# Self-attention on one core: the softmax denominators of a unit move from the front of the next unit's first run of 32-column products to the back of its second run

## The chip, the cores and the metric

The kernel runs on one core of a Trainium2 chip. The core has a matrix engine (TensorE, PE in the profile, with its weight loads shown apart as PEld), a vector engine (DVE), an activation engine (ACT), a general engine (GpSimd, POOL), and DMA queues, most of them issued by SyncE (SPq) and some by ACT (ACTq). The engines run side by side, each takes its own instructions in order, and they wait for one another through semaphores. The metric is the time on the device in microseconds (us), the median of several executions; lower is better. Before the change it is 2229.88 us, the median of three runs (2228.8 to 2230.53).

## The reference, cut to what matters

Four sequences of 1024 tokens and 512 channels go through a decoder layer (causal self-attention, cross-attention over 64 context tokens, a feed-forward part) and then through a gated fusion. The change touches only the causal self-attention, which has 16 heads of 32 channels:

```python
xn1 = _ln(x, g1, be1)
q, k, v = ...                                  # 16 heads of 32 channels
scores = jnp.einsum('bhtd,bhsd->bhts', q, k) / scale       # scale = 32 ** -0.5
scores = jnp.where(mask, scores, -jnp.inf)                 # causal
attn = jax.nn.softmax(scores, axis=-1)
out  = jnp.einsum('bhts,bhsd->bhtd', attn, v)
```

A softmax row is exp(score - row maximum), divided by its sum. The kernel applies that division late: it first multiplies the exponentials with v, and separately adds the exponentials over all keys; that sum is the denominator.

## The kernel before, in words

**Units.** Self-attention is cut into 32 units: 4 sequences, times 4 groups of 4 heads, times 2 sets of 4 query tiles (a tile is 128 queries, so a unit has 512 query columns). In sequence 0, group 0, the two sets are tiles 0 to 3 and 4 to 7; everywhere else they are (0, 1, 6, 7) and then (2, 3, 4, 5), so two kinds of units take turns. In this text the first is the *wide* kind (it looks at 8 key blocks of 128 keys) and the second the *middle* kind (6 key blocks).

**What a unit does.** `maxima` (products `s`, L673) finds row maxima ahead of time. `attend` then handles the key blocks `kb` in a hand-written order (`o7` = 0, 7, 2, 1, 3, 6, 4, 5 for the wide kind, `o5` = 0, 5, 1, 4, 2, 3 for the middle kind). For each block `exps` makes the scores again, transposed (TensorE, tile `st`, L729, in a PSUM pool of three banks), takes exponentials on ACT into SBUF tiles `pT` (L734; the first block's go to two of the four `total` buffers, the others to a ring of seven), and, for a block on the diagonal, zeroes the masked half on POOL with affine_select (L742). A block `kb` covers only the query columns that may see it, from `first_col[kb]` to 512: in the wide kind 512 columns for block 0 and 128 for block 7; in the middle kind 512 for block 0 and 128 for block 5.

**The runs of 32-column products.** Every two blocks, `weigh_all` (L747) multiplies the exponentials with v: four products per block, one per head, each with a stationary operand of 32 columns and up to 512 moving columns (`av`, L759). A product appears as two matmul records in the trace, because the operands are float32. These products are kept together: the first is the *lead*, and the others are tied to come behind it on TensorE and get a high priority (`issue_after`, `high_priority`), so that they normally form one run. After each run POOL adds the blocks' exponentials into the first block's tiles (`weigh`, L783): `held[0]` is both the operand of the first block's products and the accumulator, so the first add of a unit has to wait until those products have read it. When the last block has been added, `held[0]` holds the sums over keys.

**The denominators.** `sums` (L791) makes, for unit u, four more 32-column products with a stationary matrix of ones (`den`, L796), which add `held[0]` over the 128 partitions, into a bank of the `st` pool; then `end` copies the bank to SBUF on ACT (`dens`, L801) and sends it to DRAM by SyncE's queue (`dend`, L804). `attend` returns `sums` as the next unit's `tail`. In the kernel before, unit u+1's first run calls it: the denominators of unit u lead, and the run's own products come behind them. The last unit's denominators are made alone at the end of the phase.

**What sets the order.** `run` (L114) merges three streams of steps (a unit's own steps, the maxima of the units ahead, and the projections of later sequences as filling) by the share that is left of each, and gives each stream a priority. When the program is built, a planner turns this list into one fixed order per engine with its own estimates of when things are ready: on each engine it takes the ready instruction of the highest priority. The chip then runs each engine's order as it is and waits where an operand is late. So a change of one run's lead may change where many other instructions stand.

Of the kernel before, what the change touches and what calls it, by code (L numbers as in the profile page):

```python
# [28 lines left out]
HG = P // DH  # L29
# [22 lines left out]
def decoder_then_fusion(ctx: ExitStack, tc: tile.TileContext, x, ctxT, cols, rows,  # L52
# [385 lines left out]
    def self_attention(ph):  # L438
# [99 lines left out]
        def columns(tiles, n):  # L538

            at = [j for j, tile in enumerate(tiles) if tile // NJ == n]  # L540
            if not at:
                return None
            first = tiles[at[0]] % NJ
            return slice(at[0] * P, (at[-1] + 1) * P), slice(first * P, (first + len(at)) * P)
# [74 lines left out]
        order = list(range(KST))  # L619
# [89 lines left out]
        def attend(u, tail):  # L709


            b, g, h, tiles = units[u]

            order = Z["o%d" % tiles[-1]] if tiles[0] != 4 else Z["o9"]
            first_col = [P * sum(tile < kb for tile in tiles) for kb in range(tiles[-1] + 1)]
            last = order[-1]
            held = {}

            def exps(kb, r, m):

                c0 = first_col[kb]
                w = TG - c0
                if r == 0:
                    tag, bufs = ("total", 4) if kb == order[0] else ("pT", None)
                    held[kb] = [ptp.tile([P, 2, TG], F32, tag=tag, name=f"pT_{u}_{kb}_{i}", bufs=bufs)
                                for i in range(2)]
                st = ps_of["st"][0].tile([P, m, w], F32, tag=ps_of["st"][1], name=f"st_{u}_{kb}_{r}")
                for i in range(m):
                    nc.tensor.matmul(st[:, i], k_at[u, kb // NJ][:KM, r + i, (kb % NJ) * P : (kb % NJ + 1) * P],  # L729
                                     q_at[u][:KM, r + i, c0:], start=True, stop=True)  # L730
                for i in range(0, m, 2):
                    k = min(m, 2)
                    at = (r + i) % 2
                    nc.scalar.activation(held[kb][(r + i) // 2][:, at : at + k, c0:], st[:, i : i + k], AF.Exp,  # L734
                                         scale=-QSCALE)

                done = r + m
                for i in range(HG // 2):
                    if kb in tiles and r < 2 * i + 2 <= done:
                        t = held[kb][i][:, :, c0 : c0 + P]  # L740
                        if i < Z["mp"]:
                            nc.gpsimd.affine_select(out=t, in_=t, compare_op=ALU.is_ge, fill=0.0, base=0,  # L742
                                                    pattern=[[0, 2], [1, P]], channel_multiplier=-1)
                        else:
                            nc.vector.tensor_tensor(t, t, reach.unsqueeze(1).to_broadcast([P, 2, P]), ALU.min)

            def weigh_all(kbs):  # L747

                if kbs[0] == order[0]:
                    held["av"] = ps_av.tile([P, TG], F32, tag="av", name=f"av_{u}")  # L750
                    todo = [(kb, r) for kb in kbs for r in range(HG)[::-1]]
                else:
                    todo = [(kb, r) for kb in kbs[::-1] for r in range(HG)[::-1]]
                if kbs[-1] == last:
                    todo = [(kb, r) for kb in sorted(kbs, key=lambda k: k == last) for r in range(HG)[::-1]]

                def one(kb, r):
                    c0 = first_col[kb]
                    return nc.tensor.matmul(held["av"][r * DH : (r + 1) * DH, c0:],  # L759
                                            v_at[b, g][:, kb, r * DH : (r + 1) * DH],  # L760
                                            held[kb][r // 2][:, r % 2, c0:], start=kb == order[0], stop=kb == last)
                if kbs[0] == order[0] and tail:
                    lead, others, end = tail()
                    others += [lambda at=at: one(*at) for at in todo]
                else:
                    lead, *others = [lambda at=at: one(*at) for at in todo]
                    end = lambda: None
                first = lead().ins
                with tc.issue_after(first), tc.high_priority(offset=Z["hp"]):
                    for product in others:  # L770
                        product()
                end()
                for kb in kbs:
                    weigh(kb)

            def weigh(kb):
                c0 = first_col[kb]
                if kb != order[0]:

                    spare = u + Z["spf"] - len(units)  # L780
                    for i, (t, p) in enumerate(zip(held[0], held[kb])):
                        eng = nc.vector if i and (u == 1 and kb in Z["dv1"] or spare >= 0 and (kb % 2 or spare > 1) or spare < 0 and kb in Z["dv"]) else nc.gpsimd
                        eng.tensor_tensor(t[:, :, c0:], t[:, :, c0:], p[:, :, c0:], ALU.add)  # L783
                if kb == last:
                    avs = outp.tile([P, TG], F32, tag="avs", name=f"avs_{u}", bufs=1)
                    nc.scalar.copy(avs, held["av"])
                    for n in range(NG):
                        if shared := columns(tiles, n):
                            nc.sync.dma_start(av_dram[b, n, g][:, shared[1]], avs[:, shared[0]])

            def sums():  # L791

                den = ps_of[Z["den"]][0].tile([P, TG], F32, tag=ps_of[Z["den"]][1], name=f"den_{u}")

                def product(r):
                    return nc.tensor.matmul(den[r * DH : (r + 1) * DH, :], ones, held[0][r // 2][:, r % 2, :],  # L796
                                            start=True, stop=True)

                def end():
                    dens = outp.tile([P, TG], F32, tag="dens", name=f"dens_{u}", bufs=1)  # L800
                    nc.scalar.copy(dens, den)  # L801
                    for n in range(NG):
                        if shared := columns(tiles, n):
                            nc.sync.dma_start(den_dram[b, n][g * HG : (g + 1) * HG, shared[1]],  # L804
                                              dens[::DH, shared[0]])

                first, *others = [lambda r=r: product(r) for r in range(HG)[::-1]]
                return first, others, end

            groups_of = [order[i : i + Z["grp"]] for i in range(Z["grp0"], len(order), Z["grp"])]  # L810
            if Z["grp0"]:
                groups_of.insert(0, order[: Z["grp0"]])
            due = {sum(len(a) for a in groups_of[: i + 1]) - 1 + Z["lag"]: a for i, a in enumerate(groups_of)}

            steps = []
            for i in range(len(order) + Z["lag"]):
                if i < len(order):
                    kb = order[i]
                    w = TG - first_col[kb]
                    m = TG // w if w <= TG // 2 else 1  # L820
                    steps += [(m * w, lambda kb=kb, r=r, m=m: exps(kb, r, m)) for r in range(0, HG, m)]
                if i in due:
                    kbs = due[i]
                    steps.append((4 * sum(TG - first_col[kb] for kb in kbs), lambda kbs=kbs: weigh_all(kbs)))
            return steps, sums
# [77 lines left out]
        tail, first_late = None, len(units) - AHEAD  # L903
        for u in range(len(units)):
            if u and u + 2 < len(units):
                load_stacks(u + 2, u)
            main, tail = attend(u, tail)
# [4 lines left out]
            if u and u + 2 < len(units) and Z["phi%d" % n]:  # L912
                begun = maxima(u + 2)
                k = Z["phi%d" % n]
                first = begun[: k]
# [11 lines left out]
            else:  # L927
                fill = pieces[u + AHEAD]
            run(main, ahead, fill, speed=(Z["main"], (Z["ahead%d" % n] if u < Z["alf"] else Z["ahead_l"]) if u else Z["a0"], Z["fill"]), sooner=(Z["so0"], Z["so1"], Z["so2"]))
        first, others, end = tail()  # L930
        first()
        for product in others:
            product()
        end()
        switch(None)()
# [613 lines left out]
    for phase in (self_attention, cross_attention, feed_forward):  # L1549
        with ExitStack() as ph:  # L1550
            phase(ph)
# [41 lines left out]
```

## Time and profile before

| what | value |
|---|---|
| median of the runs | 2229.88 us |
| the profiled execution's own time | 2229.15 us |
| its span, first to last instruction | 2227.4 us |
| mean granted TensorE clock | 0.981 |
| PE busy over the span | 2121.6 us (95%) |
| POOL busy over the span | 1070.6 us (48%) |
| the stretch in which unit denominators are made (115 to 970 us) | 855.0 us |
| PE / DVE / ACT / POOL busy in it | 811.4 / 560.6 / 442.4 / 666.0 us |
| denominator products | 256 records, 114.2 to 969.0 us |
| copies of the denominators on ACT | 32, 586 ns each (median) |
| their DMAs in that stretch | 58 of 4 KB and 2 of 8 KB |

The busy time of an engine is the time its instructions took; the rest is idle. The idle time before a group of instructions is put down to whatever ended it (the releaser). TensorE's matmuls overlap, and their ends are modelled, so the distance between the starts of two matmuls tells their price better than their durations do. A waits view lists, for an engine and a line, whom it waited for: total us, how many times, the longest. In a timeline, `x8` means that eight records in a row were merged into one line, and the second column is the time from the first start to the last end.

### The profile page before, as it was taken

How to read it: one execution, taken by the hardware profiler on the slowest of the kernel's cores; microseconds unless marked ns; L12 is line 12 of the kernel's file. 1: busy time of each engine (PE TensorE's matmuls, PEld its weight loads, DVE VectorE, ACT ScalarE, POOL GpSimd, SP SyncE). 2: the span in 40 equal slices, each digit the busy share in tenths (PEclk: the TensorE clock that was granted, in tenths of full speed). 3: DMA queues.
4: the chain of work that ended last, by engine and by line, in shares of the span. 5: the costliest groups of instructions: out<-in, count | busy, mean ns of one | idle time of the engine just before them, and what ended most of it. 6: DMA issues, size and time to landing. Idle time of an engine off the chain costs nothing.

```text
span 2227.4 us, 34074 instructions
## 1 busy us (share of the span) xinstructions
PE 2121.6 (95%) x11736; PEld 1606.5 (72%) x11736; DVE 1255.2 (56%) x2800; ACT 983.7 (44%) x2175; POOL 1070.6 (48%) x1139
## 2 busy tenths in 40 slices
PE   6899999999999999989999998999999999999997
PEld 5667665666666755558888886888887887888785
DVE  6566756765665578666677756341337225431727
ACT  3355545554655455435555565432233324232432
POOL 3178777787878778765555523010115103410414
PEclk9999999999999999999999999999999999999998
DMA  8856766676656467662323214644345525442631
GB/s 251 241 157 172 238 194 206 192 221 191 192 151 189 136 168 221 201 205 67 101 80 104 80 50 154 197 166 141 124 139 207 170 98 202 145 175 85 207 134 48
DMA packets 219427, 356.24 MB, mean 160 GB/s; under 512 B 33516, under 2 KB 101852, under 8 KB 217206
## 3 DMA queue, kind: packets, MB, share of 16 engines
q1 hardware_dynamic: 201548, 333.83, 48.0%
q10 hardware_dynamic: 17706, 20.24, 2.9%
q8 instruction: 93, 1.52, 0.3%
q14 instruction: 80, 0.66, 0.1%
HBM read 242.27 MB, written 111.18 MB: 159 GB/s over the span
## 4 chain that ended last, share of the span: by engine, by line
PE 67%; DMA 10%; DVE 10%; issue 6%; POOL 4%; ACT 3%; SPq 1%; DVEq 0%; ACTq 0%; POOLq 0%
PE ph_f L101 13%; PE acc_f L1331 13%; PE s L673 4%; PE st L729 4%; PE av L759 4%; PE po_c L101 3%; PE pq_x L101 3%; PE pk L101 3%; PE pg_o L101 3%; PE pq L101 3%; PE po_x L101 3%; POOL pT L783 3%; PE pv L101 2%; PE sc_c L86 2%; PE den L796 1%
## 5 line engine op out<-in xcount | busy, mean ns | idle before, releaser
L783 POOL TENSOR_TENSOR pT<-pT,pT 128x256 f32<-128x256 f32 (+3 forms) x369 | 547.4, 1504 | 98.4 <-PE av L759 85.0
L1331 PE MATMUL acc_f<-wf,hs_f 128*128 128x512 f32 x1536 | 384.9, 394 | 7.6 <-DVE hs_f L74 5.9
L734 ACT ACTIVATE pT<-st 128x512 f32<-128x512 f32 (+2 forms) x640 | 317.2, 561 | 158.0 <-PE st L729 101.3
L101 PE MATMUL ph_f<-xn_f,wf 128*128 128x512 f32 x1536 | 381.7, 393 | 3.3 <-DVE xn_f L74 2.6
L1331 PEld LDWEIGHTS acc_f<-wf,hs_f 128*128 128x128 f32 x1536 | 285.0, 188 | 71.0 <-DVE hs_f L74 8.1
L101 PEld LDWEIGHTS ph_f<-xn_f,wf 128*128 128x128 f32 x1536 | 287.8, 189 | 65.0 <-DVE xn_f L74 3.0
L678 DVE CUSTOM_DVE_ANT_0 s<-s,mask 128x512 f32<-128x512 f32 (+3 forms) x512 | 245.8, 502 | 118.8 <-PE s L673 118.0
L673 PE MATMUL s<-ks,qs 96*128 96x512 f32 (+3 forms) x768 | 250.8, 375 | 28.4 <-DVE top L681 8.3
L1310 ACT ACTIVATE ph_f<-ph_f,colv 128x512 f32<-128x512 f32 x128 | 84.4, 659 | 391.3 <-PE ph_f L101 387.2
L74 DVE TENSOR_TENSOR hs_f<-ph_f,hs_f 128x512 fp32r<-128x512 f32 x128 | 87.9, 686 | 285.6 <-ACT hs_f L73 285.6
L729 PE MATMUL st<-qs,ks 98*128 98x256 f32 (+2 forms) x888 | 231.1, 342 | 12.2 <-DMA qs<-mT 6.6
L681 DVE TENSOR_REDUCE top<-s 128x1 f32<-128x512 f32 x256 | 175.6, 686 | 108.5 <-PE s L673 108.1
L673 PEld LDWEIGHTS s<-ks,qs 96*128 96x128 f32 x768 | 140.5, 194 | 107.3 <-DVE top L681 23.1
L729 PEld LDWEIGHTS st<-qs,ks 98*128 98x128 f32 x888 | 150.0, 193 | 65.3 <-ACT pT L734 24.7
L1306 POOL TENSOR_TENSOR y_f<-y_f,row_bf 128x512 f32<-128x512 f32 x32 | 42.0, 1317 | 313.8 <-DMA y_f<-x 253.9
L742 POOL TENSOR_SCALAR_AFFINE_SELECT pT<-pT 128x256 f32<-128x256 f32 x256 | 106.0, 431 | 126.1 <-ACT pT L734 92.6
L759 PE MATMUL av<-pT,v 128*32 128x512 f32 (+3 forms) x1776 | 157.2, 455 | 5.1 <-POOL pT L742 4.6
L1446 POOL TENSOR_TENSOR g_o<-g_o,z_o 128x512 f32<-128x512 f32 x28 | 41.8, 1506 | 175.7 <-DVE g_o L1445 172.9
L101 PE MATMUL pv<-wv,xn_s 128*128 128x256 f32 x768 | 107.5, 290 | 6.7 <-ACT vout L578 5.4
L101 PEld LDWEIGHTS pv<-wv,xn_s 128*128 128x128 f32 x768 | 100.4, 194 | 18.3 <-ACT vout L578 6.0
L1082 POOL TENSOR_TENSOR p_c<-p_c,inv_c 128x512 f32<-128x512 f32 x64 | 68.8, 1076 | 87.1 <-DVE inv_c L1081 65.2
L101 PE MATMUL pk<-xn_s,wk 128*128 128x512 f32 x384 | 104.0, 412 | 1.6 <-ACT xn_s L73 0.8
(220 smaller groups left out, 3397.0 us busy)
## 6 DMA issues: line engine op xcount, KB each, us to landing
wf<-wf2d SPq DMA_DIRECT2D x84, 512.0 KB
ks<-kd SPq DMA_DIRECT2D x96, 256.0 KB
qs<-qd SPq DMA_DIRECT2D x96, 256.0 KB
kd<-k SPq DMA_DIRECT2D x64, 256.0 KB
qd<-q SPq DMA_DIRECT2D x120, 128.0 KB
wf<-wf1d SPq DMA_DIRECT2D x28, 512.0 KB
x<-in_x SPq DMA_DIRECT2D x32, 256.0 KB
wk<-wk SPq DMA_DIRECT2D x16, 512.0 KB
```

Of the source, the lines that this page charges most:

```text
L74: (lo_eng or nc.vector).tensor_tensor(lo, src, hi, ALU.subtract)
L101: nc.tensor.matmul(held["ps"], a_at(a()[i], c), b_at(b()[j], c), start=not bias and c == 0 and k == 0, stop=c == NC - 1 and k == 2)
L673: nc.tensor.matmul(sc[:, :w], q_at[u][:KS, r, j * P : (j + 1) * P], k_at[u, m][:KS, r, :w], start=True, stop=True)
L678: nc.vector.tensor_tensor_reduce(sc[:, :w], sc[:, :w], mask[:, TG - w :], 1.0, TOP, ALU.add, ALU.min, dst)
L681: nc.vector.tensor_reduce(dst, sc, AX.X, ALU.min)
L729: nc.tensor.matmul(st[:, i], k_at[u, kb // NJ][:KM, r + i, (kb % NJ) * P : (kb % NJ + 1) * P], q_at[u][:KM, r + i, c0:], start=True, stop= ...
L734: nc.scalar.activation(held[kb][(r + i) // 2][:, at : at + k, c0:], st[:, i : i + k], AF.Exp, scale=-QSCALE)
L742: nc.gpsimd.affine_select(out=t, in_=t, compare_op=ALU.is_ge, fill=0.0, base=0, pattern=[[0, 2], [1, P]], channel_multiplier=-1)
L759: return nc.tensor.matmul(held["av"][r * DH : (r + 1) * DH, c0:], v_at[b, g][:, kb, r * DH : (r + 1) * DH], held[kb][r // 2][:, r % 2, c0: ...
L783: eng.tensor_tensor(t[:, :, c0:], t[:, :, c0:], p[:, :, c0:], ALU.add)
L1310: nc.scalar.activation(ps, ps, AF.Relu, bias=col("bf1", f))
L1331: mm = nc.tensor.matmul(acc[j], held[f][i0][:, j * P : (j + 1) * P], w[2, f][:, i1], start=f == 0 and m == 0, stop=last and m == 2)
```

## The change

Unit u's denominators are no longer made with unit u+1's first run. `weigh_all` now calls `tail` when it reaches the run that begins with `order[Z["grp"]]`, the third block in the order, which is the second run; the four denominator products are appended to that run's products, so the run's own first product leads and the denominators come last. The copy and the DMAs of the denominators (`end`) move with them. The first run is now led by its own first product: block 0, head 3. `sums` returns one list of products instead of a first one and the others; the four products at the end of the phase stay what they are.

```diff
@@ in weigh_all @@
-                if kbs[0] == order[0] and tail:
-                    lead, others, end = tail()
-                    others += [lambda at=at: one(*at) for at in todo]
-                else:
-                    lead, *others = [lambda at=at: one(*at) for at in todo]
-                    end = lambda: None
+                sums, end = tail() if kbs[0] == order[Z["grp"]] and tail else ([], lambda: None)
+                lead, *others = [lambda at=at: one(*at) for at in todo] + sums
                 first = lead().ins
                 with tc.issue_after(first), tc.high_priority(offset=Z["hp"]):
                     for product in others:
@@ in sums @@
-                first, *others = [lambda r=r: product(r) for r in range(HG)[::-1]]
-                return first, others, end
+                return [lambda r=r: product(r) for r in range(HG)[::-1]], end
@@ at the end of the phase @@
-        first, others, end = tail()
-        first()
-        for product in others:
+        sums, end = tail()
+        for product in sums:
             product()
         end()
```

## The prediction

> **What bounds the kernel now.** I read the busy table by stretches first, then the waits between 115 and 970 us (where the denominators are made), then TensorE's and POOL's timelines around a few first runs, and last the clock at one stall. The busy table for that stretch, and for its best and worst 100 us (columns: stretch, length, busy us and count for PE, PEld, DVE, ACT, POOL, then clock, DMA share, GB/s):
>
> ```profile
> 115.00:970.00 855.00, 811.39 (x5181) 543.08 (x5174) 560.64 (x1521) 442.38 (x881) 665.97 (x670) 0.98 0.65 189
> ```
> ```profile
> 700.00:800.00 100.00, 99.56 (x670) 68.80 (x669) 60.79 (x186) 51.48 (x104) 80.50 (x81) 1.00 0.55 153
> 800.00:900.00 100.00, 90.33 (x521) 58.44 (x519) 80.39 (x186) 54.00 (x108) 80.97 (x72) 0.91 0.72 207
> ```
>
> TensorE is the bound: 811.4 of 855.0 us, so 43.6 us idle in all; POOL is at 78%. The waits of the same stretch:
>
> ```profile
> POOL pT L783 <- PE av L759: 81.9, 27, 7.6
> POOL pT L742 <- ACT pT L734: 75.4, 29, 6.3
> ...
> PEld st L729 <- ACT pT L734: 23.4, 47, 2.7
> ...
> PEld av L759 <- POOL pT L742: 14.0, 31, 0.8
> ...
> PE st L729 <- ACT pT L734: 5.0, 3, 2.4
> PE av L759 <- POOL pT L742: 4.6, 12, 0.6
> ```
>
> and, from the waits of TensorE alone:
>
> ```profile
> PE den L796 <- POOL pT L783: 2.1, 1, 2.1
> ```
>
> The reader sees that the large waits stand on POOL, which has slack: its first add of a unit waits for the unit's first `av` run, 81.9 us in 27 units, 3.0 us each. TensorE's own waits on exponentials and masks are small: 5.0 + 4.6 us, and 2.1 for a denominator. How one wait of the first kind looks, on POOL and then on TensorE, in a middle unit:
>
> ```profile
> 502.19 0.77 POOL L742 TENSOR_SCALAR_AFFINE_SELECT pT<-pT 128x256 f32<-128x256 f32 x2 [0.25 <-ACT pT L734]
> 508.06 3.90 POOL L783 TENSOR_TENSOR pT<-pT,pT 128x256 f32<-128x256 f32 x3 [5.10 <-PE av L759]
> ```
> ```profile
> 502.84 2.92 PE L101 MATMUL pq<-xn_s,wq 128*128 128x512 f32 x12
> ...
> 505.99 1.07 PE L796 MATMUL den<-pT,ones 128*32 128x512 f32 x8
> 506.87 1.26 PE L759 MATMUL av<-pT,v 128*32 128x512 f32 x16
> 508.06 0.61 PE L673 MATMUL s<-ks,qs 96*128 96x256 f32 x2
> ```
>
> The masks were done at 502.96, the last add of the unit before at 501.94; TensorE did 2.9 us of projection and then denominators plus `av`. It was never idle: POOL's 5.10 us were free of charge.
>
> **The price of a run.** Starts on TensorE's timeline, at full clock, to the start of the next other matmul:
>
> ```profile
> 583.12 1.05 PE L796 MATMUL den<-pT,ones 128*32 128x512 f32 x4
> 584.10 0.50 PE L673 MATMUL s<-ks,qs 96*128 96x512 f32 x1
> ...
> 586.36 1.06 PE L759 MATMUL av<-pT,v 128*32 128x512 f32 x8
> 587.35 0.45 PE L729 MATMUL st<-qs,ks 98*128 98x384 f32 x1
> ...
> 588.08 0.43 PE L759 MATMUL av<-pT,v 128*32 128x128 f32 x8
> 588.43 0.33 PE L673 MATMUL s<-ks,qs 96*128 96x128 f32 x1
> ```
>
> Four products of 512 columns take 0.99 us alone, of 128 columns 0.35. So 384 columns are worth 0.64 us, 512 are worth 0.85, and 0.99 - 0.85 = 0.14 us is a fixed price per run. The 505.99 run tests it: 512 + 512 + 128 columns give 0.14 + 1.92 = 2.06; its starts are 2.07 apart. The denominators thus cost 0.85 us in any run, and moving them costs nothing in itself; what counts is how many runs there are.
>
> **The change part by part.** Sum against the profiled execution's own 2229.15 us (span 2227.4 and 1.75 around it), which is 0.73 under the median of 2229.88.
>
> 1. *Four denominator products, 31 times, from the first run to the second.* 31 x 0.85 us leave one place and appear in the other: 0. Where the `st` bank they need is not free when the second run is issued, they become a run of their own: 0.14 each. Before, 4 of the 31 already stand apart from the `av` products, which are then a run. Bounds 0 - 4 x 0.14 = -0.6 and 27 x 0.14 = +3.8; I take half, +1.6.
>
> 2. *The first run has a new lead.* Before, the denominators' lead needed a free `st` bank and the previous unit's finished sums; by then both blocks of the first run were usually ready in the 16 middle units (one run), while in the wide units block 7 stood apart by itself (0.35 us). Now the lead is block 0's own product, which can be placed as soon as block 0 is ready, so that block 5 of the middle units falls behind: 16 x 0.14 = +2.2 at worst; joined in the 15 wide units instead, -2.1. In a middle unit block 0 needs no mask and block 5 does, which favours the split: +1.1.
>
> 3. *The first run loses a cover.* The 0.85 us of denominators let POOL's masks of the new unit finish while TensorE was busy. Those masks often end right at that time (for the denominators at 480.80 the last one of the batch ends at 480.95). The other 126 or so runs have no such cover, and TensorE's wait for a mask is 4.6 us in 12 cases, 0.4 each. By their rate the 31 first runs pay 31 x 12/126 x 0.4 = 1.2; if every one lost the whole cover, 31 x 0.85 = 26. Below nothing is excluded, since the old wait for POOL's sums is counted in 4. The nearest row is the 0.4 us of one wait; I take it in 10 of the 31 units, +4.0, because the masks of the wide units are the last things to come. What is queued behind such a wait is all of TensorE's order, `st` and `s` first.
>
> 4. *POOL starts a unit's adds sooner.* Up to 81.9 us of POOL's waiting can go. POOL was off the path, so what TensorE gets is only its own waits on this chain: 5.0 + 4.6 + 2.1 = 11.7 us at most, and nothing at least, because the `st` waits I looked at come with ACT held up by a DMA (ACT's 0.5 to 4.3 us waits of `vout` for `vd`). I take -1.5.
>
> 5. *What moves with the denominators.* One ACT copy of 0.59 us per unit, later by the distance of the two runs (5 to 10 us), and two DMAs of 4 KB on SyncE's queue, past the loads and stores issued in that time. SyncE already waits 28.8 us for these copies with its later transfers queued behind. Nobody needs the values within 10 us: the inverse is read two units after a sequence's last unit. The `held[0]` buffers are four, two units' worth, so they too have 10 us to spare. 0; without that cover, a late stack load stalls TensorE by what its longest such wait shows, 3.5 us (`s` for `qd`, in the waits of the whole span).
>
> 6. *The fixed order is planned anew.* Every lead that moves shifts the work around it. TensorE's idle time per 100 us varies from 0.4 to 9.7 us in the present order with the same kinds of work. I take +2 for the following: a stall also costs clock. Bounds -8 and +12, an estimate from that spread, as no row prices a new order.
>
> The clock, shown by the stall at 531 us (columns as in the first table):
>
> ```profile
> 528.60:531.60 3.00, 0.78 (x5) 0.47 (x4) 1.27 (x4) 1.73 (x4) 0.00 (x0) 1.00 0.25 96
> 531.60:535.60 4.00, 3.88 (x18) 1.03 (x18) 1.77 (x6) 2.08 (x5) 1.13 (x3) 0.60 0.84 306
> ```
>
> A 2.24 us wait is followed by a granted clock of 0.60, and denominators plus 512 columns took 3.43 us instead of 1.85: 1.6 us on top of the stall. So two new stalls of this size would cost 7.7 us by the row. The Trainium skill, "TensorE: Matmul & The Clock Gate", section "Why this matters for your kernels", asks only that gaps stay under about 3 us. By that rule two 2.24 us stalls would cost 4.5 us and no clock; this trace disagrees with it, and the trace decides.
>
> Sum: 1.6 + 1.1 + 4.0 - 1.5 + 0 + 2 = +7.2 on 2229.15, that is 2236.4, or 2237 beside the median. I forecast 2236, a little slower (+0.3%).
>
> **The rivals.**
>
> *Faster: POOL's earlier start pays.* The first run needs no sums of the unit before, POOL adds up to 3.0 us sooner, ring buffers come free, and the waits of step 4 go (-11.7), with one clock drop (-1.6), at an unchanged number of runs and +2.5 for masks: -10.8, so 2219. For it: POOL at 78% and its chain of adds before the third run of a unit. Against: TensorE has other work in nearly all of those waits. It decides if `PE av` waits on masks do not grow.
>
> *No change.* TensorE does the same matmuls at 95% busy; runs are joined as often as split, new mask waits and lost old ones cancel. 2230, within about 0.2% (4.5 us), which is what a measurement of this kernel can tell from no change. Against: the lead's condition really changes in every unit.
>
> *Clearly slower: the first run is placed too early in all units.* The plan takes block 0 as ready before POOL has masked it, TensorE stops at the lead, up to 0.85 us in 31 units (26 us), with splits at their upper bounds (+6.0) and little gain: +22 to +30, about 2255. It decides from some 0.5 us of wait per unit on. Against: the 12 present waits are at most 0.6 us.
>
> **How the numbers follow.** My forecast (own range 2232 to 2243) 0.40; faster 0.22; no change 0.22; clearly slower 0.16. A sixth of the first lies within 0.2% (under 2234.3): 0.06. So faster 0.22, same 0.28, slower 0.50. The range cuts off about a tenth at each end: 2220 to 2253, which takes in most of the faster case and the lower part of the clearly slower one.
>
> **What would show it.** Right: POOL's wait of L783 on `av` falls well under 81.9 us while PE's busy time stays near 811; the runs of 32-column products, counted on TensorE's timeline, grow from 157 to between 160 and 190; some denominators stand alone; `PE av` waits on L742 rise from 4.6 towards 9 us. Wrong: the number of runs falls, or the `st` waits on ACT go away (faster); or a new wait of TensorE on `s` or `st` of over 10 us appears, which no step here has (slower). It would also be wrong if the plan leaves the first runs where they are.

## The result and the profile after

The changed kernel takes 2246.3 us (median of four runs, 2245.01 to 2252.06) against 2229.34 us before: a ratio of 1.0081, 95% interval 1.0063 to 1.0100. It is slower by 17 us. The forecast was 2236: the direction was right, the size less than half of what came.

The profiled execution after took 2245.01 us, span 2243.2, so 15.9 us more than the one before. All of it is lost before cross-attention's score products begin: their first one (`sc_c`) starts at 989.1 us before and at 1005.9 after, 16.8 us later, and the later phases nearly keep that distance (the last `acc_f` starts 15.8 us later). The table of busy time from the start to that point, before and after (columns: stretch, length, busy us and count for PE, PEld, DVE, ACT, POOL, then clock, DMA share, GB/s):

```profile
0.00:989.10 989.10, 914.75 (x5709) 625.27 (x5709) 638.61 (x1706) 490.27 (x969) 707.10 (x738) 0.97 0.67 195
```
```profile
0.00:1005.90 1005.90, 932.97 (x5709) 630.51 (x5710) 635.35 (x1706) 488.86 (x969) 707.49 (x738) 0.96 0.66 192
```

TensorE does the same 5709 matmuls. Its idle time is 989.10 - 914.75 = 74.4 us before and 72.9 after: the change added no idle time. Its busy time grew by 18.2 us. The mean granted clock over the whole span tells most of the reason:

```profile
core 0: 2227.4 us, clock 0.981
```
```profile
core 0: 2243.2 us, clock 0.976
```

The missing clock is worth (1 - 0.981) x 2227.4 = 42.3 us before and (1 - 0.976) x 2243.2 = 53.8 us after: 11.5 of the 15.9 us. The rest, 4.4 us, is what this rough sum doesn't hold (the clock is printed to three digits, one digit of the last place being 2.2 us).

How clock is lost, in the profile after. First the wait on TensorE, at the start of a projection, then the clock in the 3.4 us before it, in the 3.4 us from it on, later, and in the 3.4 us from 613.90 on:

```profile
611.07 0.50 PE L729 MATMUL st<-qs,ks 98*128 98x512 f32 x1 [0.28 <-ACT pT L734]
613.18 4.61 PE L101 MATMUL pk<-xn_s,wk 128*128 128x512 f32 x12 [1.61 <-DVE xn_s L74]
```
```profile
609.40:612.80 3.40, 1.89 (x12) 0.64 (x11) 1.65 (x3) 3.40 (x8) 3.28 (x3) 1.00 1.01 322
613.20:616.60 3.40, 3.40 (x9) 2.64 (x10) 3.40 (x11) 0.74 (x2) 1.12 (x3) 0.60 0.25 83
617.00:620.40 3.40, 3.40 (x20) 1.99 (x19) 2.21 (x6) 2.21 (x5) 2.06 (x6) 0.95 0.45 133
613.90:617.30 3.40, 3.40 (x10) 2.62 (x9) 3.40 (x11) 0.04 (x1) 1.66 (x5) 0.50 0.12 36
```

A wait of 1.61 us costs itself and then a stretch at half the clock (the last row, 0.50; the 0.60 of the second row is a mean over a window that begins earlier): the twelve projection products take 4.5 us from their first start to the start of the next matmul, while twelve of them took 2.75 us at full clock in the profile before (502.84 to 505.59). TensorE's waits of 1.5 us and more are 8 between 115 and 970 us before and 10 between 115 and 985 us after, mostly in other places; two of the new ones are `pk` for `xn_s`, here and at 394 us, a wait that is at most 0.8 us in the profile before.

The waits of the same stretch as before (115 us to the phase's end), after the change:

```profile
POOL pT L742 <- ACT pT L734: 147.7, 49, 7.6
...
ACT dens L797 <- PE den L792: 75.3, 28, 8.0
...
POOL pT L779 <- PE av L759: 28.0, 30, 2.6
...
PE st L729 <- ACT pT L734: 7.3, 8, 3.2
```
```profile
PE av L759 <- POOL pT L742: 2.2, 5, 0.5
```

POOL's wait for the first run fell from 81.9 to 28.0 us, as the change's mechanism says; its wait for exponentials rose instead, from 75.4 to 147.7, so POOL gained nothing lasting. TensorE's wait for masks did not grow, it fell from 4.6 to 2.2 us. New, and not in the prediction, is ACT: it stood 12.6 us in front of the copy of the denominators before (the row below) and stands 75.3 us after.

```profile
ACT dens L801 <- PE den L796: 12.6, 20, 1.9
```

SyncE's queue does the same with their DMAs:

```profile
SPq L804 <- ACT dens L801: 28.8, 18, 4.7
...
SPq L804 <- ACT pT L734: 14.0, 4, 4.6
```
```profile
SPq L800 <- ACT dens L797: 57.0, 13, 8.8
SPq L800 <- ACT pT L734: 39.3, 14, 8.5
```

The first pair is before, the second after: 42.8 us and 96.3 us. Behind it on that queue stand, among others, the loads of `x` that `xn_s` needs.

### The profile page after: what moved, and what is told of

The parts are those of the page before. It is cut to its first block, busy times and chain, and to the rows that moved or that the text cites. A ratio compares the mean times of both kernels' runs of the same rounds, so it can differ in the third digit from the quotient of the medians.

```text
span 2243.2 us, 34083 instructions
## 1 busy us (share of the span) xinstructions
PE 2139.6 (95%) x11736; PEld 1611.5 (72%) x11736; DVE 1254.5 (56%) x2800; ACT 982.7 (44%) x2175; POOL 1070.4 (48%) x1139
## 4 chain that ended last, share of the span: by engine, by line
PE 72%; DVE 9%; DMA 9%; issue 5%; POOL 2%; ACT 2%; SPq 1%; DVEq 0%; ACTq 0%; POOLq 0%
PE ph_f L101 12%; PE acc_f L1325 12%; PE av L759 5%; PE st L729 4%; PE s L673 4%; PE po_c L101 4%; PE pq_x L101 4%; PE po_x L101 4%; PE pk L101 3%; PE pq L101 3%; PE pg_o L101 3%; PE pv L101 3%; PE sc_c L86 2%; PE av_c L1097 2%; DVE s L678 2%
## 5 line engine op out<-in xcount | busy, mean ns | idle before, releaser
L779 POOL TENSOR_TENSOR pT<-pT,pT 128x512 f32<-128x512 f32 (+3 forms) x369 | 545.0, 1501 | 39.4 <-PE av L759 31.2
L673 PE MATMUL s<-ks,qs 96*128 96x512 f32 (+3 forms) x768 | 255.6, 378 | 29.4 <-DVE top L681 9.4
L759 PE MATMUL av<-pT,v 128*32 128x512 f32 (+3 forms) x1776 | 167.6, 470 | 2.3 <-POOL pT L742 2.2
L101 PEld LDWEIGHTS pv<-wv,xn_s 128*128 128x128 f32 x768 | 103.3, 198 | 15.9 <-DVE top L678 4.6
L101 PE MATMUL pk<-xn_s,wk 128*128 128x512 f32 x384 | 108.6, 426 | 4.4 <-DVE xn_s L74 3.4
```

Of the source, the lines that this page charges most:

```text
L101: nc.tensor.matmul(held["ps"], a_at(a()[i], c), b_at(b()[j], c), start=not bias and c == 0 and k == 0, stop=c == NC - 1 and k == 2)
L673: nc.tensor.matmul(sc[:, :w], q_at[u][:KS, r, j * P : (j + 1) * P], k_at[u, m][:KS, r, :w], start=True, stop=True)
```

## The experiments

Three theories stood at the start. *Blocked queues*: the denominators' copy and DMAs stand too early in ACT's and SyncE's orders, and what is behind them comes late. *Early first run*: the first run, led by its own block 0, is split and placed too early. *New order*: the planner's order simply came out with worse stalls, and any small disturbance may do that.

### Which part of the change costs

The change does two things: it takes the denominators from the lead of the first run, and it puts them at the back of the second. Two kernels do one without the other, and two controls change only the pace that the merge of the streams gives to a unit's own steps, which changes no work but makes the planner draw a new order.

e1, the denominators lead the second run (against the changed kernel):

```diff
-                lead, *others = [lambda at=at: one(*at) for at in todo] + sums
+                lead, *others = sums + [lambda at=at: one(*at) for at in todo]
```

> The denominators go to the second run, but lead it (the first run is led by its own block 0, as after the change). Three theories. BLOCKED QUEUES: the loss comes from the denominators' copy and DMAs, planned earlier than the denominators really end, so that ACT and SyncE stand in order behind them (ACT's wait for denominators 12.6 us before, 75.3 after; SyncE's 42.8 before, 96.3 after). A lead is placed only when its operands and bank are ready, so here ACT's wait should fall under 30 us and the time to within 5 us of before (2229 to 2235). EARLY FIRST RUN: the first run led by its own product is what costs (splits and early placing): the time stays at 2243 to 2249. NEW ORDER: the loss is only that the fixed order came out worse, with stalls in other places; then the time may be anything from 2225 to 2250 and does not follow ACT's wait.

Measured: 2222.3 us, ratio to before 0.9957 (0.9941 to 0.9973). Faster than before.

e2, the denominators behind the first run's products (against the changed kernel):

```diff
-                sums, end = tail() if kbs[0] == order[Z["grp"]] and tail else ([], lambda: None)
+                sums, end = tail() if kbs[0] == order[0] and tail else ([], lambda: None)
```

> The denominators stay with the first run but come behind its products, so that the first run is led by its own block 0. BLOCKED QUEUES: as after the change, the denominators are no lead, ACT's wait for them should be 40 us or more and the time 2238 to 2250. EARLY FIRST RUN: the lead is that of after, the time 2243 to 2249. NEW ORDER: anything from 2225 to 2250, not following ACT's wait.

Measured: 2221.1 us, ratio 0.9957 (0.9942 to 0.9973). Faster too, and ACT waited 36.0 us for the denominators.

e3 and e4, the kernel before with another pace:

```diff
-'main': 1.0,
+'main': 0.98,        # e3;  1.02 in e4
```

> The kernel before, with the pace of a unit's own steps in the merge at 0.98 in place of 1.0: no work changes, only the order is planned anew. NEW ORDER: the time moves by a good part of the 17 us, either way (beyond 5 us). BLOCKED QUEUES and EARLY FIRST RUN: the denominators lead as before, so within 5 us of 2229.

> The kernel before with that pace at 1.02: a second control. NEW ORDER: the time moves by more than 5 us in at least one of the two controls. BLOCKED QUEUES and EARLY FIRST RUN: within 5 us of 2229.

Measured: e3 2233.7 us, ratio 1.0010 (0.9996 to 1.0024); e4 2243.0 us, ratio 1.0060 (1.0041 to 1.0080).

What follows: *early first run* falls. Both kernels whose first run is led by its own block 0 are faster than before, by 0.43%. And *new order* is real: e3 stays where the kernel before is, but e4, which changes no work and no arrangement either, loses three quarters of what the change lost, again with a lower clock:

```profile
core 0: 2242.1 us, clock 0.976
```

### Are the differences more than a drawn order?

The same two paces for the changed kernel and for e1.

> The changed kernel with the pace of a unit's own steps at 0.98: same work, order planned anew. After the first four runs EARLY FIRST RUN has fallen. Two theories stand. NEW ORDER: the place of the denominators means nothing; each planned order draws its stalls, and this kernel may fall anywhere from 2220 to 2250, near 2233 as likely as near 2246. BLOCKED QUEUES: denominators behind the second run hold up ACT (75 us of waits) and SyncE (103 us) in any order, so this kernel stays above 2240 and ACT's wait above 50 us.

> The changed kernel at 1.02. NEW ORDER: anywhere from 2220 to 2250, and the two kernels of this pair differ by 8 us or more from each other or from 2246. BLOCKED QUEUES: above 2240, ACT's wait for denominators above 50 us.

> Denominators leading the second run (2222.3 us at 1.0), at pace 0.98. NEW ORDER: anywhere from 2220 to 2250. BLOCKED QUEUES: ACT's wait stays under 30 us and the time stays under 2230.

> The same at pace 1.02. NEW ORDER: anywhere from 2220 to 2250. BLOCKED QUEUES: under 2230, ACT's wait under 30 us.

Measured: e5 2230.3 us, e6 2247.2, e7 2220.4, e8 2222.8.

And later, with the last four, a second order of e2's arrangement:

> The denominators behind the first run's products (2221.1 us at pace 1.0), at pace 1.02, a second order of the same arrangement. If the arrangement counts, within 6 us of 2221 as the three kernels with leading denominators were of one another; NEW ORDER alone: anywhere from 2215 to 2250.

Measured: e12 2218.9 us.

| where unit u's denominators stand | pace 0.98 | pace 1.0 | pace 1.02 |
|---|---|---|---|
| lead of the first run (before) | 1.0010 (0.9996 to 1.0024) | 1 | 1.0060 (1.0041 to 1.0080) |
| back of the second run (the change) | 1.0009 (0.9989 to 1.0030) | 1.0081 (1.0063 to 1.0100) | 1.0077 (1.0050 to 1.0105) |
| lead of the second run (e7, e1, e8) | 0.9952 (0.9931 to 0.9974) | 0.9957 (0.9941 to 0.9973) | 0.9957 (0.9941 to 0.9972) |
| back of the first run (e2, e12) | not run | 0.9957 (0.9942 to 0.9973) | 0.9959 (0.9944 to 0.9974) |

All are ratios to the kernel before on the same chip. So both hold: an arrangement's time moves by 0.6 to 0.7% with a mere new order in the first two rows (e5, the changed kernel at another pace, equals the kernel before), and yet the last two rows are faster in all five kernels and agree within 0.07%. At each pace, denominators at the back of the second run cost 0.6 to 1.2% more than the same denominators leading it. Against the kernel before at the same pace, the change costs nothing at 0.98, 0.8% at 1.0 and 0.2% at 1.02: the 17 us are those of one pair of orders, not of the change as such. *Blocked queues* had said that e5 stays above 2240 us; it came to 2230.3, with 58.8 us of ACT's wait. It had also said 2238 to 2250 us for e2, which is fast. e6 (66.7 us of ACT's wait), e7 and e8 were what it said, and so were the short waits of ACT in e1, e7 and e8 (14 to 19 us); e1 came out faster than its 2229 to 2235. SyncE's wait, counted as above, is 64 to 66 us in e1, e7 and e8, more than the 42.8 before, though these kernels are faster. Both waits needed a direct test.

### Taking the two new waits away

e9, the copy on ACT is tied behind the first exponential of the sixth block:

```diff
+                    done_exp = nc.scalar.activation(...).ins         # in exps, the same instruction
+                if held.get("end"):
+                    with tc.issue_after(done_exp):
+                        held.pop("end")()
...
-                end()                                                # in weigh_all
+                held["end"] = end if sums else None
```

> The changed kernel with one more tie: ACT's copy of the denominators stands behind the first exponential of the sixth block, so that it is issued later on ACT and the denominators are done by then. BLOCKED ACT (what the denominators at the back of the second run cost beside leading it, 0.6 to 1.2%, is ACT standing in front of the copy): ACT's wait for denominators falls from 76 us to under 35 and the time to 2220 to 2232. NEW ORDER alone: anywhere from 2220 to 2250. If the wait falls and the time stays above 2240, ACT's wait is not the cause.

Measured: 2251.7 us, ratio 1.0096 (1.0071 to 1.0122). The view of the `dens` copies and ACT's largest waits, in e9:

```profile
its engine sat idle before it (us, times) until:
  PE den L795: 1.6, 1
```
```profile
ACT pT L734 <- PE st L729: 161.3, 118, 7.8
```

and ACT's largest waits in the changed kernel, over the same stretch (60 to 1010 us):

```profile
ACT dens L797 <- PE den L792: 76.1, 29, 8.0
ACT pT L734 <- PE st L729: 68.0, 86, 2.8
```

The wait for denominators is gone, 76.1 to 1.6 us, and ACT waits for scores instead: 68.0 to 161.3 us. SyncE's wait at L803 for the copies is down to 13.8 us as well. The time did not fall, so neither wait is shown to cost anything. ACT was ahead of TensorE in any case, and the copy only happened to be the instruction at which it stood. This is one order, and a new order alone moves the time by 0.7%; but e2 and e12, with 36.0 and 39.2 us of ACT's wait against 12.6 before, say the same.

e10, the DMAs of the denominators on ACT's queue:

```diff
-                            nc.sync.dma_start(den_dram[b, n][g * HG : (g + 1) * HG, shared[1]],
+                            nc.scalar.dma_start(den_dram[b, n][g * HG : (g + 1) * HG, shared[1]],
```

> The changed kernel with the two DMAs of the denominators issued by ACT, right behind its own copy, so that SyncE's queue has no wait for them (103 us after the change). BLOCKED SYNCE: the loads of x behind that wait come in time and the time falls to 2220 to 2232, with ACT's wait still above 50 us. BLOCKED ACT: the time stays above 2240, or rises by ACT's two issues (about 1 us per unit, off the path).

Measured: 2253.9 us, ratio 1.0114 (1.0086 to 1.0142). SyncE has no wait in front of these DMAs any more, ACT's wait is 78.8 us, and the time is no better. By itself this is again one order; with e1, e7 and e8, where SyncE waits longer than before and the time is shorter, SyncE's wait does not account for the loss either.

e11, the copy on DVE:

```diff
-                    nc.scalar.copy(dens, den)
+                    nc.vector.tensor_copy(dens, den)
```

> The changed kernel with the copy of the denominators on DVE. BLOCKED ACT: ACT has no wait for denominators; the time falls to 2220 to 2235 unless DVE's own wait for them (up to some 60 us) delays the row maxima. BLOCKED SYNCE or NEW ORDER: no reason to fall; 2240 or more is as likely as not.

Measured: 2240.2 us, ratio 1.0037 (1.0019 to 1.0055). This is better than the change by about 0.4%, which is within what a new order does; alone it decides nothing. DVE waits 33.6 us for the denominators, and ACT 169.0 us for scores.

### What does go with the time

I counted, on TensorE's timeline, the runs of 32-column products and those that last over 1.8 us from their first start to the start of the next other matmul.

| kernels | ratio | runs | denominators in a run of their own / with `av` products | runs over 1.8 us |
|---|---|---|---|---|
| before, e3, e4 | 1 to 1.006 | 157 to 159 | 8 to 9 / 28 | 31 to 32 |
| after, e5, e6, e9, e10, e11 | 1.0009 to 1.0114 | 168 to 173 | 1 to 3 / 30 to 31 | 31 to 34 |
| e1, e7, e8 | 0.9952 to 0.9957 | 188 | 29 / 3 | 10 |
| e2, e12 | 0.9957 to 0.9959 | 179 to 182 | 17 / 15 to 16 | 13 |

A run is counted alone when it holds denominators only; the 9 of the kernel before are all of two products, so that a unit's denominators make two of them. In all 14 kernels the number of long runs parts the fast from the rest. It does not part the change from the kernel before. How a wide unit's second run looks in the changed kernel and in e1, on TensorE's timeline:

```profile
523.19 1.50 PE L759 MATMUL av<-pT,v 128*32 128x256 f32 x16
524.50 1.04 PE L792 MATMUL den<-pT,ones 128*32 128x512 f32 x8
525.48 0.61 PE L673 MATMUL s<-ks,qs 96*128 96x128 f32 x2
```
```profile
498.63 1.06 PE L792 MATMUL den<-pT,ones 128*32 128x512 f32 x8
499.62 0.50 PE L673 MATMUL s<-ks,qs 96*128 96x512 f32 x1
499.96 0.34 PE L729 MATMUL st<-qs,ks 98*128 98x384 f32 x1
```

In the changed kernel no score product stands between 523.19 and 525.48, 2.29 us; in e1 the denominators go by themselves, 0.99 us, scores for DVE and ACT follow at once, and the run's `av` products come only at 501.83. And the middle of the phase, 200 to 800 us, after, before and in e1:

```profile
200.00:800.00 600.00, 572.36 (x3707) 390.27 (x3706) 372.45 (x1075) 309.73 (x624) 455.57 (x470) 0.97 0.63 182
```
```profile
200.00:800.00 600.00, 573.08 (x3805) 395.30 (x3805) 381.46 (x1109) 319.44 (x641) 467.53 (x484) 0.98 0.65 187
```
```profile
200.00:800.00 600.00, 580.97 (x3884) 396.00 (x3882) 386.72 (x1143) 326.79 (x651) 480.46 (x495) 1.00 0.66 192
```

In the same 600 us TensorE finished 3707, 3805 and 3884 matmuls, and every other engine less or more work with it; the clock is 0.97, 0.98 and 1.00.

The clock is not the whole of it. The lost clock, (1 - clock) x span, is 45 to 46 us in the kernel before (mean over the runs of each comparison). It is 53.9 us in the changed kernel, 54.6 in e4 and 57.9 in e9, but only 49.9 in e6, which is as slow as the change, and 42.5 and 43.8 in e2 and e12, which gained about 10 us each, 4 us or less of it clock. So what the two fast arrangements save is in part something else, which stays open.

The long runs are a link, not a proof. That a long run starves DVE and ACT, and that the stalls and lost clock come from there, is argued only: the ten waits of 1.5 us and more in the profile after, between 115 and 985 us, begin 4.8 to 24.9 us after the last long run (one run that is long only by the wait behind it left aside). A run that joins or parts the denominators with everything else in place could not be had, because every edit makes the planner draw a new order.

## Why the prediction was right or wrong

Right: slower, and inside the range. Wrong: the size, 17 us instead of 7, and for the most part the reasons. That the sign came out is partly luck, since at pace 0.98 the same change costs nothing. Of the signs that were to show the forecast right, POOL's wait fell and the runs rose from 157 to 168; but PE's busy time did not stay near 811 us (826.5 between 115 and 985 us), no moved denominators stand alone, and `PE av` waits did not rise.

1. *Moved denominators, +1.6.* They were expected to stand alone in half of the cases; of the 31 moved, none does. The row at 583.12 was also misread: its four records are two products, not four, and they took 0.98 us, as long as the four products at 586.36. So a unit whose denominators fall into two halves pays nearly twice. Before, three units did so (the prediction counted four units apart; the fourth, at 905 us, is so in part), after none. All runs of 32-column products together took 187.2 us before and 188.4 after. Without what the low clock added (6.4 and 11.1 us, counted in the traces' clock record) they took 180.9 and 177.3: with step 2, -3.6 us where +2.7 was taken.

2. *New lead of the first run, +1.1.* 31 of 32 first runs are now split, as feared (18 before): `av` of block 0, then other matmuls, then `av` of the second block. But e1 and e2 are split too (30 and 31) and are faster, so the split by itself does not make a kernel slow. Using the price of 0.14 us as the whole cost of a run was the mistake: fewer runs are cheaper by that price, yet the kernels with 179 to 188 runs are the fast ones.

3. *Lost cover, +4.0.* This failed. `PE av` waits on masks fell from 4.6 to 2.2 us. The largest term of the sum was for a wait that did not come.

4. *POOL's earlier start, -1.5.* The mechanism came as described (81.9 to 28.0 us) and, as argued, gave TensorE next to nothing in the changed kernel: its three waits of that chain were 11.7 us and are 9.5 (7.3 + 2.2 + 0). Whether it is what makes e1 and e2 faster than before stays open; they have it too (29.9 and 32.9 us, over 60 us to the phase's end), but so has the changed kernel.

5. *Copy and DMAs, 0.* The prediction knew of SyncE's wait but not that it would grow, and had no wait of ACT: they stand in front of the DMAs and the copy for 96 and 75 us. The zero stands as far as is shown: e9 and e10 took these waits away and gained nothing.

6. *New order, +2.* This is the mis-sized term. It was given bounds of -8 and +12 and a middle of +2; the other terms measured together come to about -6 (-3.6 for steps 1 and 2, -2.2 for the waits of steps 3 and 4), and this one, as what is left of 15.9 us, to about +22, of which some 11.5 us are clock. It cannot be foreseen from the rows of one order: e4 and e5 show that the same arrangement moves by 13 to 17 us with the pace. The prediction did price a lost clock step (1.6 us per stall, by the row at 531 us) but counted next to none. The trace after agrees with that row: a wait of 1.61 us was followed by a clock of 0.50 for 3.4 us. That wait is well under the gap of about 3 us that the Trainium skill, "TensorE: Matmul & The Clock Gate", section "Why this matters for your kernels", allows; the measurement decides.

The rivals: *clearly slower* named the wrong place (the first run's lead) and a price of 22 to 30 us; *faster* did not happen to this kernel, but its time of 2219 us is what the five kernels of e1's and e2's kind reach (2219 to 2223), with more runs rather than as many; *no change* is what e5 shows for the same arrangement at another pace.

## What to carry to other kernels

When a planner fixes the order, measure a change in more than one order before believing its sign: a pace changed by 2% moved this kernel by up to 0.7% with no work changed. What held in every order tried here was that the denominators are better as the lead of the second run or at the back of the first (0.9952 to 0.9959 of the time before, versions that beat both kernels). Why is not shown; that it is because few long runs are left is only a link. And a wait that grows on an engine that is ahead anyway, like ACT's 75 us, need not cost anything; take it away in an experiment before blaming it.

## What the runs showed of the hardware

In the profiled pair the loss went through busy time and not through idle time: the same 5709 matmuls took 18.2 us more while idle time fell by 1.4 us, and some 11.5 us of that is lost clock; the rest is not explained. In the traces' clock record the clock is 1.00 or 0.50 and nothing between, and in the profile after every stretch at 0.50 in the phase lasts 3.41, 6.83 or 10.24 us. A wait of 1.61 us was enough for one. Of the ten waits of 1.5 us and more between 115 and 985 us, nine end within 1.1 us of the start of such a stretch; the tenth, 1.73 us at 318 us, has none. Three further stretches (at 122, 494 and 901 us) begin without a single wait of over 0.93 us. At 242 us a longer stall of TensorE is followed by the double length:

```profile
238.80:242.20 3.40, 0.02 (x1) 0.00 (x0) 3.40 (x6) 0.77 (x2) 3.40 (x6) 0.95 1.07 321
242.20:248.60 6.40, 6.32 (x28) 2.08 (x28) 3.77 (x11) 0.97 (x3) 5.54 (x5) 0.50 0.16 41
248.60:252.00 3.40, 3.40 (x26) 2.27 (x26) 1.67 (x4) 0.64 (x3) 2.62 (x3) 0.99 0.01 2
```

For 6.4 us the clock is 0.50, though TensorE is busy again for nearly all of it; in the 3.4 us after that it is 0.99 (the stretch itself lasts from 241.85 to 248.68 us).
